# A graph layer's streamed table in six buffers of four blocks instead of three of five, with 12 instead of 16 buffers for gathered rows

## The chip, the cores and the metric

The kernel runs on one core of one Trainium2 chip. The metric is the device time of one execution in microseconds. Before the change, three runs gave 1752.2, 1746.14 and 1751.6 us, a median of 1751.6 us.

The engines are named as the profile names them: PE is TensorE (PEld its weight loads), DVE is VectorE, ACT is ScalarE, POOL is GpSimd, SP is SyncE, which here only issues DMAs.

## What is computed

There are 12,500 nodes with 128 features and 200,000 edges, sorted by destination; every edge has one of four types. The reference, cut to what matters:

```python
h = jnp.maximum(_layernorm(x, axis=-1), 0.0)
xs = h[src]
msgs = jnp.zeros((xs.shape[0], W.shape[2]), dtype=x.dtype)
for i in range(W.shape[0]):
    mask = (edge_type_4 == i)[:, None]
    msgs = msgs + jnp.where(mask, xs @ W[i] + b[i], 0.0)
out = x + jax.ops.segment_sum(msgs, dst, num_segments=N)
```

## The kernel before

**The table.** The first 110 us normalize x and write h into a table `htab` in DRAM, as three bf16 parts per value, so that a row has 384 bf16 (768 bytes). Partition p of a tile holds 98 consecutive rows (NW = 98), and "block j" is row j of all 128 partitions: 128 x 128 values in three parts, 98,304 bytes. The rows of x are loaded in 33 spans of up to three blocks by `load_span` (L472). Its tiles come from the pool `rows` (L234, 16 buffers of 1,536 bytes per partition). `load_span` is asked up to 13 spans ahead of the one that is normalized (L1240).

**Two kinds of edges.** The edges are cut into 1,563 chunks of 128. The first 512 chunks go to the few destinations with many edges and are treated as dense work. The other 1,051 go through gathers.

- *Gathered chunks.* For each chunk POOL issues one indirect DMA that fetches 128 rows of `htab` (L544). Two chunks share a tile `hm` of the same pool `rows` (HG = 2). Chunks are worked in groups of 16: `gather` (L538) asks for the rows of the next group while `sum_up` (L569) multiplies those of the present one (L578, three matmuls per chunk), sums by weights (L605), and DVE adds the result into a ring in SBUF (L666). The first 48 chunks take another path (rows of x itself, L528), so 1,003 gathers go through `rows`.
- *Dense work.* Destinations are handled in 18 batches: the first of 17 triples of nodes, then 17 of 27 triples. `count` (L940) counts, for a batch, how often each row of the table is a source: DVE makes one-hots (L959, L967), PE multiplies them (L985), ACT copies the finished count of each triple out of PSUM (L991). `multiply` (L1024) then multiplies the counts of the batch with the whole table: 98 blocks of three matmuls (L1040).

**The stream.** `multiply` reads the table from DRAM once per batch, HB blocks to a DMA on SP (L1032), into the pool `hsp` of STREAM buffers (L1290). With HB = 5 that is 20 DMAs per batch, 19 of 480 KB and one of 288 KB, 360 in all. Besides waiting for its buffer, each DMA is made to wait for a copy of `count`: the first ACT copy that PE's order puts behind the last matmul on that buffer.

```python
for j0 in range(0, NW, HB):
    j1 = min(j0 + HB, NW)
    hs = hsp.tile([P, HB, D3], BF16, name="hs")
    one = nc.sync.dma_start(hs[:, : j1 - j0, :], htab.rearrange("(p j) f -> p j f", j=NW)[:, j0:j1, :])
    free = [by for n, by in left_at if n > by_blocks[0] - STREAM]
    if free and by_blocks[0] >= STREAM:
        held_by(one, free[0], "the buffer of the stream is free")
```

`by_blocks` counts the buffers that PE is through with, and `left_at` holds each copy with the value of `by_blocks` at which it was emitted.

**The order.** From group 3 on, the order on PE, DVE and ACT is written out by hand (L1311 to L1400). Between two pairs of gathered chunks, `pace` (L1088) hands out steps of the dense work so that all groups have about the same number of matmul columns. `dense_work` (L1103) runs the count of a batch beside the multiplication of the batch before; multiplication is kept 15% behind (BEHIND, L1122), so at the end of a batch the last blocks run without a count beside them, and a new batch begins with 15% of its count before its first block of the other is multiplied:

```python
done = {st: 0.0 for st in steps}
while done:
    st = min(done, key=lambda st: done[st] + led.get(st, 0.0))
    part = next(st, None)
```

`multiply` yields after every block whatever HB is. POOL and SP each work through their own queue in order.

Of the kernel before, what the change touches and what calls it, by code (L numbers as in the profile page):

```python
# [55 lines left out]
C0 = 512  # L56
UB = 27
MANY = 16
HB = 5
SLOTS = 4  # L60
SETS = 4
STREAM = 3
BEHIND = 0.15
RING = 2048
OT = 4
# [9 lines left out]
def kernel(  # L75
# [155 lines left out]
    flag = const.tile([P, 1], I32, name="flag")  # L231

    mid = ExitStack()
    hpool = mid.enter_context(tc.tile_pool(name="rows", bufs=16))  # L234
    opool = mid.enter_context(tc.tile_pool(name="onehots", bufs=2))
    spool = mid.enter_context(tc.tile_pool(name="typed", bufs=2))
    x_ps = mid.enter_context(tc.tile_pool(name="x_ps", bufs=4, space=PSUM))
# [279 lines left out]
    def held_by(one, by, reason):  # L517
        tc.add_manual_dep(
            one.ins,
            by.name,  # L520
            mybir.DependencyInfo(mybir.DependencyClass.Sync, mybir.DependencyReason.DATA),
            reason=reason,
        )
# [14 lines left out]
    def gather(t0, g):  # L538
        got = []
        for h0 in range(0, g, HG):  # L540
            hm = hpool.tile([P, HG * D3], BF16, name="hm")
            for i in range(h0, min(h0 + HG, g)):
                at = (t0 + i) % (TURN * P)
                one = nc.gpsimd.indirect_dma_start(  # L544
                    out=hm[:, (i - h0) * D3 : (i - h0 + 1) * D3],
                    out_offset=None,
                    in_=htab,
                    in_offset=bass.IndirectOffsetOnAxis(ap=srcf[:, at : at + 1], axis=0),
                )
                if i == h0 and gates and t0 + i >= SOON:  # L550
                    held_by(one, gates.pop(0), "the first rows come while the slots are made, not ahead of them")
            got.append(hm)
        return lambda i, c: got[i // HG][:, (i % HG * 3 + c) * D : (i % HG * 3 + c + 1) * D]
# [470 lines left out]
    def multiply(vs, counts):  # L1024
# [3 lines left out]
        pa = a_ps.tile([P, 512], F32, name="pa")  # L1028
# [7 lines that stand above are left out]
# [253 lines left out]
    nc.vector.memset(o2s[:, :, :, NB:], 1.0)  # L1289
    hsp = counting.enter_context(tc.tile_pool(name="hsp", bufs=STREAM))  # L1290
    raw_sums = outp.tile([P, OT, D], F32, name="xo").rearrange("p j d -> p (j d)")[:, : RAW * G * win_raw]
# [14 lines left out]
    rows = gather(RAW * G, G)  # L1306
# [6 lines left out]
    for gi, (t0, g) in list(enumerate(zip(starts, sizes)))[RAW:]:  # L1313
# [11 lines left out]
        if gi < final:  # L1325
            rows = gather(starts[gi + 1], sizes[gi + 1])
# [203 lines left out]
```

## Time and profile before

The profiled execution took 1744.29 us; its span from the first to the last instruction is 1742.5 us. Its mean granted TensorE clock is 0.926.

| part of the span, us | what runs |
|---|---|
| 0 to 112 | x is normalized, the table is written, slots for the dense work are made |
| 112 to 190 | the first 48 chunks, the first count |
| 190 to 1690 | gathered groups, with count and multiplication between them |
| 1690 to 1742 | last groups, results leave |

| engine | busy us (share) | instructions |
|---|---|---|
| PE | 1435.4 (82%) | 10984 |
| DVE | 1015.9 (58%) | 5305 |
| ACT | 450.0 (26%) | 1095 |
| POOL | 1031.1 (59%) | 1078 |

The view of the costliest groups of instructions gives a line, engine and operation, its number, the busy time and mean duration of one, then the idle time of the engine just before them and what ended it. The view of waits gives, for each pair "who <- whom", the idle time in total, how many times, and the longest. "issue" there is idle time for whose end the profile shows no event. The chain that ended last follows the work back from the last instruction; "SPq" is SP issuing a DMA.

### The profile page before, as it was taken

Reading aid. Unit: us, or ns where it says so; the run is one execution under the profiler, and the core shown is the slowest. Engines: PE = TensorE matmul, PEld = TensorE weight load, DVE = VectorE, ACT = ScalarE, POOL = GpSimd, SP = SyncE. Lnnn points to the kernel's source line nnn. Section 1 sums busy time; section 2 is a strip of 40 time slices with the busy share of each in tenths; the row PEclk is TensorE's granted clock in tenths of the full one; section 3 lists DMA queues with packets and bytes.
Section 4 is the critical chain, followed back from the end, with each engine's and each line's share of the span. In section 5 each row is a group of like instructions: output and inputs, shape, how many; then the busy total and the mean of one; then the engine's idle time right before and its main releaser. Section 6 shows DMA issues by size and latency. Waiting matters only on the chain.

```text
span 1742.5 us, 32539 instructions
## 1 busy us (share of the span) xinstructions
PE 1435.4 (82%) x10984; PEld 938.3 (54%) x10984; DVE 1015.9 (58%) x5305; ACT 450.0 (26%) x1095; POOL 1031.1 (59%) x1078
## 2 busy tenths in 40 slices
PE   3876779787979787888888889888888989889875
PEld 1345565554656455555555555555555556555554
DVE  6972867565565556574647555756564556555334
ACT  5783322121212121212121222222222222122011
POOL 6536656565656565656665656666656566656561
PEclk8976799998999899999999999999999899999997
DMA  6542466565646465666555555655555655556652
GB/s 204 179 146 81 144 196 188 173 208 169 196 158 206 158 197 169 206 187 193 175 188 189 175 183 174 200 181 187 178 190 169 197 173 189 173 179 188 196 185 67
DMA packets 144538, 308.92 MB, mean 177 GB/s; under 512 B 26762, under 2 KB 77372, under 8 KB 144365
## 3 DMA queue, kind: packets, MB, share of 16 engines
q1 hardware_dynamic: 94685, 204.98, 35.9%
q0 software_dynamic: 49680, 101.81, 19.9%
q8 instruction: 86, 1.41, 0.3%
q14 instruction: 87, 0.71, 0.1%
HBM read 290.65 MB, written 16.04 MB: 176 GB/s over the span
## 4 chain that ended last, share of the span: by engine, by line
PE 52%; issue 19%; DMA 14%; DVE 5%; another core or an unknown queue 4%; ACT 4%; SPq 2%; DVEq 0%; ACTq 0%
PE pa L1040 27%; DMA hs<-htab 14%; PE pt L985 8%; PE py L605 5%; PE ps L578 4%; ACT counts L991 2%; PE pt L1056 2%; SPq L1032 1%; PE ps L635 1%; DVE oh L561 1%; PE py L596 1%; PE pt L691 1%; DVE o L967 1%; ACT sb L581 1%
## 5 line engine op out<-in xcount | busy, mean ns | idle before, releaser
L544 POOL DMA_INDIRECT hm<-htab,srcT x1003 | 974.6, 972 | 642.5 <-issue 227.1
L1040 PE MATMUL pa<-counts,hs 128*128 128x324 fp8e4 (+1 forms) x5292 | 970.4, 309 | 195.1 <-DMA hs<-htab 150.7
L1040 PEld LDWEIGHTS <-hs 128*128 128x128 bf16 x5292 | 490.9, 98 | 478.1 <-DMA hs<-htab 187.3
L959 DVE TENSOR_SCALAR o<-iota_n,hkT 128x392 bf16<-128x392 f16 x1167 | 381.3, 327 | 97.7 <-PE pt L985 44.1
L985 PE MATMUL pt<-o,o 128*128 128x396 bf16 x1167 | 374.9, 345 | 23.2 <-issue 10.4
L991 ACT CAST counts<-pt 128x396 int32<-128x396 f32 x476 | 230.0, 493 | 555.8 <-PE pt L985 306.3
L561 DVE TENSOR_SCALAR oh<-iota_b,keyT 128x56 bf16<-128x56 bf16 (+8 forms) x1003 | 171.5, 258 | 328.9 <-PE py L596 89.8
L581 ACT COPY sb<-ps 128x224 f32<-128x224 f32 (+8 forms) x251 | 99.7, 397 | 529.4 <-PE ps L578 237.5
L666 DVE TENSOR_TENSOR ring<-ring,py 128x14 f32 (+7 forms) x976 | 171.2, 175 | 82.5 <-PE py L605 20.8
L578 PEld LDWEIGHTS <-hm 128*128 128x128 bf16 x3009 | 166.1, 100 | 75.3 <-issue 30.1
L578 PE MATMUL ps<-oh,hm 128*128 128x56 bf16 (+8 forms) x3009 | 189.3, 199 | 18.0 <-issue 13.9
L967 DVE TENSOR_SCALAR o<-iota,loT 128x128 bf16<-128x128 bf16 x644 | 175.2, 272 | 0.0
L985 PEld LDWEIGHTS <-o 128*128 128x128 bf16 x1167 | 114.0, 99 | 77.3 <-issue 23.9
L967 DVE TENSOR_SCALAR o<-iota,loT,byT 128x128 bf16<-128x128 bf16 x417 | 139.6, 335 | 0.0
L605 PE MATMUL py<-sb,wsb 128*128 128x224 f32 (+7 forms) x488 | 130.3, 410 | 0.4 <-issue 0.3
L605 PEld LDWEIGHTS py<-sb,wsb 128*128 128x128 f32 x488 | 89.9, 197 | 24.6 <-issue 2.2
L528 POOL DMA_INDIRECT hx<-in_x_dram,srcT x48 | 50.9, 1060 | 34.1 <-issue 12.1
L1000 DVE COPY bi<-counts 128x27 int32<-128x27 int32 (+1 forms) x18 | 4.2, 232 | 106.0 <-issue 62.0
L600 ACT CAST cnt<-py 128x224 bf16<-128x224 f32 (+7 forms) x61 | 24.1, 395 | 112.4 <-PE py L596 35.2
L461 ACT ACTIVATE h<-hm,nmrt,rstdt 128x128 f32<-128x128 f32 x98 | 42.7, 492 | 2.2 <-DVE vart L446 1.9
L1056 PEld LDWEIGHTS pt<-sd,wsb 128*128 128x128 f32 x144 | 31.3, 304 | 6.9 <-ACT sd L1052 4.8
L1056 PE MATMUL pt<-sd,wsb 128*128 128x81 f32 (+1 forms) x144 | 31.0, 379 | 4.7 <-ACT sd L1052 4.7
(234 smaller groups left out, 639.6 us busy)
## 6 DMA issues: line engine op xcount, KB each, us to landing
hs<-htab SPq DMA_DIRECT2D x342, 480.0 KB
hm<-htab,srcT POOLq DMA_INDIRECT x1003
htab<-h SPq DMA_DIRECT2D x32, 288.0 KB
xo<-in_x_dram SPq DMA_DIRECT2D x23, 256.0 KB
out_dram<-xo SPq DMA_DIRECT2D x23, 256.0 KB
hs<-htab SPq DMA_DIRECT2D x18, 288.0 KB
hm<-in_x_dram SPq DMA_DIRECT2D x18, 192.0 KB
hm<-in_x_dram SPq DMA_DIRECT2D x14, 168.0 KB
```

What stands on the lines that cost most here:

```text
L544: one = nc.gpsimd.indirect_dma_start(out=hm[:, (i - h0) * D3 : (i - h0 + 1) * D3], out_offset=None, in_=htab, in_offset=bass.IndirectOffse ...
L561: nc.vector.tensor_scalar(oh[:, i, :], iota_b[:, :K], keyf[:, at : at + 1], None, ALU.is_equal)
L578: nc.tensor.matmul(ps[:, i - i0, :], rows(i, c), oh[:, i, :], start=(c == 0), stop=(c == 2))
L581: nc.scalar.copy(sb[:, i0:i1].rearrange("p g t n -> p g (t n)"), ps[:, : i1 - i0, :])
L605: nc.tensor.matmul(py[:, :g, :], wsb[:, t, :], sb[:, :g, t, :], start=False, stop=(t == NT - 1))
L666: nc.vector.tensor_tensor(to, to, of(i), ALU.add)
L959: one = nc.vector.tensor_scalar(o2[:, k, :NB], iota_n, hkT[:, s : s + 1], None, ALU.is_equal)
L967: one = nc.vector.tensor_scalar(o1[:, k], iota_1, loT[:, s : s + 1], by, ALU.is_equal, ALU.mult)
L985: one = nc.tensor.matmul(pb, o1, o2, start=first, stop=last)
L991: one = nc.scalar.copy(counts[:, :, i * NT : (i + 1) * NT], pb.rearrange("p (b t) -> p b t", t=NT))
L1040: nc.tensor.matmul(pa[:, : 3 * nu * NT].rearrange("p (m v) -> p m v", m=3), hs[:, j - j0, c * D : (c + 1) * D], of, start=(j == 0 and c == 0),
L1056: nc.tensor.matmul(py[:, : 3 * nu], wsb[:, t, :], sd[:, : 3 * nu * NT].rearrange("p (v t) -> p v t", t=NT)[:, :, t], start=(t == 0), stop= ...
```

## The change

The stream's DMAs carry four blocks instead of five, and there are six buffers for them instead of three: 25 DMAs per batch (24 of 384 KB, one of 192 KB), 450 in all. The room in SBUF per partition goes from 3 x 3,840 = 11,520 to 6 x 3,072 = 18,432 bytes. The pool `rows` has 12 buffers instead of 16, 18,432 bytes instead of 24,576: it holds 24 gathered chunks, or 12 spans of x, where it held 32 chunks or 16 spans. `STREAM` also enters the choice of the copy that a DMA waits for.

```diff
-HB = 5
+HB = 4
 SLOTS = 4
 SETS = 4
-STREAM = 3
+STREAM = 6
...
     mid = ExitStack()
-    hpool = mid.enter_context(tc.tile_pool(name="rows", bufs=16))
+    hpool = mid.enter_context(tc.tile_pool(name="rows", bufs=12))
```

## The prediction

> **What bounds the kernel now.** I read the stretch from 190 to 1690 us first, in the view of busy time by stretch (sum, then PE, PEld, DVE, ACT and POOL, granted clock, DMA share, GB/s):
>
> ```profile
> 190.00:1690.00 1500.00, 1278.01 (x10221) 845.74 (x10220) 869.01 (x4610) 330.51 (x786) 913.85 (x941) 0.95 0.58 185
> ```
>
> PE is busy for 1278 of 1500 us, DVE for 58%, POOL for 61%, the DMA engines for 58%. PE is near its bound, with 222 us idle. The waits of PE in that stretch say what for (total, times, longest):
>
> ```profile
> PE pa L1040 <- DMA hs<-htab: 150.7, 88, 8.1
> PE pa L1040 <- issue: 40.3, 46, 4.6
> PE ps L578 <- issue: 11.1, 23, 1.0
> PE pt L985 <- DVE o L967: 7.6, 3, 4.1
> ```
>
> In the trace, 180.1 us of the idle time lie directly before the first matmul on a stream buffer: the first row and most of the second. The other 42 us lie elsewhere. So the stream makes PE wait, and SP's own waits say why its DMAs come late:
>
> ```profile
> SPq L1032 <- ACT counts L991: 633.3, 146, 12.1
> ```
>
> The DMA waits for the copy that it is tied to. The chain shows it at the start of a batch (start us, duration, what):
>
> ```profile
> 665.47 1.51 PE pt L985 x9
> ...
> 668.70 0.39 ACT counts L991
> 669.09 0.02 issue
> 669.11 3.54 DMA hs<-htab
> ```
>
> The last matmul of the old batch is done at 665.47; the DMA of the next block is issued only after the new batch's first copy, at 669.11, and lands at 672.65, when PE has long run out of counting.
>
> Over all full buffers after the first 20 the trace gives these means: last matmul on a buffer to issue of the DMA that refills it 3.98 us, issue to first packet 1.36 (0.95 with nothing ahead), packets 2.24, then about 0.4 to the matmul. That is 8.0 us. With three buffers a refill has the time of two others, 2 x 1500/360 = 8.3 us. There is nothing to spare, so each late copy stalls PE.
>
> **The clock.** Of these 1500 us, 139.9 are granted at half rate, in 28 stretches. Their lengths are multiples of 3.4 us, and in the 3.4 us before each PE was idle for half of the time or more. PE worked 112 us in them, which at full rate is 56 us less; 48 us of this belongs to the 25 stretches where the idle time was a wait for the stream.
>
> The Trainium skill (TensorE: Matmul & The Clock Gate, section "HAM oscillation — how this bites in real kernels") says that gaps of over about 3.4 us are to be avoided; by it only the 13 stream waits of over 3.4 us would cost clock, by my estimate one half-rate window each, 13 x 3.4 / 2 = 22 us, and the sum below would be 26 us higher. The trace differs: the half-rate stretch at 471.2 follows a wait of 2.8 us, so I take the rows.
>
> **The change, part by part.** It is summed against the profiled execution (span 1742.5, time 1744.3).
>
> *Six buffers of four.* A refill now has the time of five others. Without its waits and the slow clock the stretch takes about 1500 - 180 - 48 = 1272 us, 2.83 us per buffer, so 14.1 us. It needs 4.0 + 1.4 + 2.24 x 4/5 + 0.4 = 7.6 us. The 6.5 us left cover most late copies (nine in ten refills now begin within 6.8 us of the release). So -180 for the waits and -48 for the clock. PE's order is the same, as `multiply` yields per block.
>
> *Starts of batches.* Counting ends when multiplication is at 85%, 83 of 98 blocks, so 20 buffers are through at the last copies. A DMA of the next batch needs a copy with at least 20, 21, 22 ... for its first, second, third buffer. So the first is free early; the second to sixth wait for the new batch's first copy, as the first three do now. By the times above, the second would be issued at 669.1 and be there at 669.1 + 0.95 + 1.8 + 0.4 = 672.2, while PE starts the first buffer by 668.7 and takes some 3 us for it (5.7 for five blocks here, at a slow clock in part): about 0.5 us late, 17 times, +9. Bounds: 0, and the present waits of some 4.5 us (+75).
>
> *90 more DMAs on SP.* An issue takes 0.32 us at the median: 450 take 144 us of 1500. SP waits for most of the stretch; nothing is added. A run of packets begins while the one ahead ends, so the 0.95 us is paid only with an empty queue.
>
> *Gathers with 12 buffers.* POOL now stays 32 chunks ahead: a gather begins 44 to 54 us before its matmul, and is held only by its buffer:
>
> ```profile
> POOL hm L544 <- issue: 212.2, 687, 0.6
> POOL hm L544 <- PE ps L578: 190.2, 107, 6.8
> ```
>
> With 24 chunks at 1.33 us (1272 us for 955) it begins some 29 us ahead, after 2 to 4 us from release to gather. Stream DMAs land within 5 us of issue even with two ahead of them; gathered rows are a fifth as large. The lead is ample. What grows is POOL's load: a gather takes 1.25 us from start to start when nothing holds it (0.95 and 0.30 of issue; mean 1.27), so POOL's 979 gathers after its first 24 take 1241 us, from 150 us on to about 1391, while PE gets to the end of the batches at about 1470. POOL is over 90% occupied and not quite the bound: +5, bounds 0 and +75 (below).
>
> *The tail.* From 1689 on, PE uses chunks 1008 to 1050 in 40 us, faster than POOL makes them. The last gather now begins at 1709.7 and is used at 1729.1. With 24 chunks, the gathers from the 1010th's release (1697.4) on run without a break: 1699 + 17 x 1.25 = 1720, landed by 1725. It still fits; 0.
>
> *Loads of x with 12 buffers.* Span u + 13 now takes the buffer of span u + 1, which is not yet normalized when it is asked for; with 16 it was that of u - 3, done before. On SP the store of span u - 2 may stand behind that load. ACT takes the store's buffer back five spans later and spans follow each other every 2.2 to 4 us, DVE is busy for 48.5 of the 50 us from 50 to 100, and the loads end with span 32. So +2; bounds 0 and +15 (21 such loads by 0.7 us, the longer issue there).
>
> *DVE and ACT* keep their work in less time: DVE goes to 68%. PE waits 7.6 us for one-hots now; +5, bounds 0 and +40 (a fivefold).
>
> Sum: 1742.5 - 180 - 48 + 9 + 5 + 2 + 5 = 1535.5, and 1.8 around the span: 1537. The median of the runs is 1751.6 where the profiled execution took 1744.3, 0.4% more, so I forecast 1544 us. Own range: 1523 without any of the additions; about 1612 with one of the two bounds of +75 taken whole.
>
> **The rivals.**
>
> - *POOL becomes the bound* (1,633 us). If PE catches up with the gathers and each pair is handed over anew, a pair takes 2.5 us and the shortest hand-over seen, 0.41: 490 pairs, 1426 us, from 150 to 1576, then some 50 us of tail and the 0.4%. For it: the load of over 90%. Against it: all gathers are ahead by dozens of chunks. 10%.
> - *The copies hold the stream still* (1,641 us): it doesn't do what it says, since every DMA is still tied to a copy, and at a batch's start five of six wait for the same one. The present waits at starts, about 4.5 us x 17 = 76, and 30 us of clock would stay: 1544 - 9 + 106. Against it: the fourth to sixth are needed 6 us and more after the first copy. 7%.
> - *Transfers go one at a time* (1,662 us). 450 x (0.95 + 1.79 + 0.4) = 1413 us from 190, then 52, and the 0.4%. Against it: the packets of buffer 124 begin at 687.00 us, those of 123 end at 687.13, so they overlap. 4%. The Trainium skill (DMA: Bandwidth & Descriptors, section "Anatomy of one DMA") gives some 2.0 us for each DMA beside its bytes, for those issued from POOL, which speaks against smaller pieces; by it, as an estimate, 450 x 2.9 us = 1305 would give about 1554.
> - *The gathers slow down* (slower than before, some 1,890 us). If denser work on DVE and the DMA engines lengthens a gather, POOL sets the end: 979 times its cadence. From 1.58 us on ((1742.5 - 195) / 979) the kernel is slower than now; at the 1.72 us that a gather and its wait take together from 200 to 250 us (29 in 50 us) it would be 150 + 1684 + 50 = 1884 and the 0.4%. For it: a gather lasted 1.2 us and more here and there. Against it: the median is 1.25 us in every stretch, with the DMA share at 0.71 (200 to 250 us) as at 0.52. 3%.
> - The forecast: 76%.
>
> **The numbers.** The range goes from 1495, where a part of the 42 us of other idle time goes too, to 1640: it holds the forecast's own range and POOL as the bound, some 84%. About 0.5% is what a measurement of this kernel can tell from no change. Faster by over 0.5%: 0.96 (all but the last rival and a little); within: 0.01; slower: 0.03.
>
> **What would show it.** Right: PE's wait at L1040 for hs under 30 us in all, the clock at 0.97 or more from 190 us to the end of the batches, PE's work there near 1225 us, a gather still 25 to 35 us ahead, stores of the table finished by 115 us. Wrong: PE waiting at L578 for DMA hm (POOL is the bound); waits at the first buffers of each batch (the copies hold); PE waiting at L985 for DVE; or the table later by more than 10 us.

## The result, and the profile after

The kernel after took 1671.46 us (median of four runs, 1668.77 to 1675.38), the kernel before 1751.9 us beside it: ratio 0.9535, 95% interval 0.9482 to 0.9587. It is faster by 80 us, where 207 were forecast, and lies outside the range. The profiled execution took 1675.38 us, its span is 1673.5 us, and the granted clock rose from 0.926 to 0.949.

First the stretch of the batches, in the same view of busy time by stretch (us, then PE, PEld, DVE, ACT, POOL, clock, DMA share, GB/s):

```profile
190.00:1600.00 1410.00, 1249.12 (x10065) 817.88 (x10064) 857.63 (x4555) 325.19 (x777) 899.77 (x924) 0.98 0.62 194
```

The clock is what I forecast (0.98, where 0.97 or more was said), and yet PE is idle for 161 of 1410 us. The waits of PE in that stretch (190 to 1620 us; total, times, longest) say for what:

```profile
PE pa L1040 <- issue: 68.8, 125, 5.5
PE ps L578 <- issue: 35.9, 61, 1.2
PE pt L985 <- issue: 17.9, 34, 1.2
PE pt L985 <- DVE o L967: 12.3, 9, 4.1
...
PE pa L1040 <- DMA hs<-htab: 4.3, 4, 2.3
```

The reader is to see two things. The wait for the stream, 150.7 us before, is 4.3: that step went as forecast. And the rows with "issue", waits for whose end the profile shows no event, are now the large ones: 68.8 us at L1040 and 35.9 at L578, against 40.3 and 11.1 before. In the chain that ended last the DMAs all but vanish (before: PE 52%, issue 19%, DMA 14%):

```profile
PE 77%; issue 11%; DVE 7%; ACT 2%; another core or an unknown queue 1%; DMA 1%; SPq 0%; DVEq 0%; ACTq 0%
```

For an account that adds up, I took from the trace the time from the first product (L1040) to the last, and split PE's idle time by what the matmul behind it waited for. "Pause" is idle time ahead of a matmul that waits for no semaphore.

| us | before | after | forecast change | change |
|---|---|---|---|---|
| first to last L1040 | 1498.7 | 1431.0 | -209 | -68 |
| waits for the stream | 182.0 | 20.1 | -171 | -162 |
| other waits, and pauses | 38.0 | 140.0 | +10 | +102 |
| of these, pauses | 26.7 | 95.1 (200 of them) | | +68 |
| PE busy | 1277.8 | 1269.6 | -48 | -8 |
| at half clock | 144.4 | 53.3 | | -91 |

So the stream's waits went, and two thirds of their time came back in other places.

PE's busy time has to be taken apart too, because a row of PE is longer than the time that its matmul adds. Rows of L1040 last 0.30 us, but at full clock and without a stop they start every 143 ns, before and after alike (medians; 32 ns at L578). So the row ahead of every stop counts some 160 ns in which PE may already stand. With each matmul put at the spacing that it has at full clock without a stop (means from e5 and e11), PE's work is the same in both kernels, and this is what its busy time holds beyond it:

| us | before | after | change |
|---|---|---|---|
| work at full clock | 1191.1 | 1191.1 | 0 |
| added by the half clock | 50.8 | 22.7 | -28 |
| rows ahead of stops | 31.4 (196 stops) | 50.2 (314 stops) | +19 |
| the rest | 4.4 | 5.6 | +1 |

The question for the chip was what the pauses are.

### The profile page after: what moved, and what is told of

The parts are those of the page before. It is cut to its first block, busy times and chain, and to the rows that moved or that the text cites. A ratio compares the mean times of both kernels' runs of the same rounds, so it can differ in the third digit from the quotient of the medians.

```text
span 1673.5 us, 32746 instructions
## 1 busy us (share of the span) xinstructions
PE 1428.9 (85%) x10984; PEld 925.3 (55%) x10984; DVE 1014.6 (61%) x5305; ACT 448.9 (27%) x1095; POOL 1031.2 (62%) x1078
## 4 chain that ended last, share of the span: by engine, by line
PE 77%; issue 11%; DVE 7%; ACT 2%; another core or an unknown queue 1%; DMA 1%; SPq 0%; DVEq 0%; ACTq 0%
PE pa L1040 44%; PE pt L985 11%; PE py L605 7%; PE ps L578 7%; DVE o L959 2%; DVE o L967 1%; PE pt L1056 1%; PE ps L635 1%; PE pt L691 1%; DVE oh L561 1%; PE py L596 1%; DVE ring L666 1%; PE ps L490 1%; DMA hs<-htab 1%
## 5 line engine op out<-in xcount | busy, mean ns | idle before, releaser
L1040 PE MATMUL pa<-counts,hs 128*128 128x324 fp8e4 (+1 forms) x5292 | 961.9, 305 | 77.1 <-issue 68.8
L1040 PEld LDWEIGHTS <-hs 128*128 128x128 bf16 x5292 | 492.5, 97 | 349.7 <-issue 123.2
L959 DVE TENSOR_SCALAR o<-iota_n,hkT 128x392 bf16<-128x392 f16 x1167 | 385.5, 330 | 79.3 <-PE pt L985 33.6
L985 PE MATMUL pt<-o,o 128*128 128x396 bf16 x1167 | 372.4, 342 | 36.8 <-issue 20.5
L991 ACT CAST counts<-pt 128x396 int32<-128x396 f32 x476 | 229.9, 495 | 470.6 <-PE pt L985 172.0
L578 PE MATMUL ps<-oh,hm 128*128 128x56 bf16 (+8 forms) x3009 | 193.1, 197 | 45.4 <-issue 38.9
L578 PEld LDWEIGHTS <-hm 128*128 128x128 bf16 x3009 | 165.1, 98 | 111.1 <-issue 66.4
L985 PEld LDWEIGHTS <-o 128*128 128x128 bf16 x1167 | 112.1, 98 | 96.9 <-issue 34.2
L490 PE MATMUL ps<-h,ident 128*128 128x384 f32 (+1 forms) x34 | 19.9, 676 | 16.0 <-issue 12.5
L1056 PE MATMUL pt<-sd,wsb 128*128 128x81 f32 (+1 forms) x144 | 25.1, 332 | 6.8 <-ACT sd L1052 5.4
```

Of the source, the lines that this page charges most:

```text
L578: nc.tensor.matmul(ps[:, i - i0, :], rows(i, c), oh[:, i, :], start=(c == 0), stop=(c == 2))
L959: one = nc.vector.tensor_scalar(o2[:, k, :NB], iota_n, hkT[:, s : s + 1], None, ALU.is_equal)
L985: one = nc.tensor.matmul(pb, o1, o2, start=first, stop=last)
L991: one = nc.scalar.copy(counts[:, :, i * NT : (i + 1) * NT], pb.rearrange("p (b t) -> p b t", t=NT))
L1040: nc.tensor.matmul(pa[:, : 3 * nu * NT].rearrange("p (m v) -> p m v", m=3), hs[:, j - j0, c * D : (c + 1) * D], of, start=(j == 0 and c == 0),
```

## Experiments

Eighteen kernels ran, on six chips that differ: the same kernel before took 1526 us on one and 1773 on another. Every ratio is to the kernel before on the same chip. A letter for a theory holds for its group of runs only (I of e1 to e3 is not I of e17).

### e1 to e4: the obvious suspects (chip with 1773 us for the kernel before)

In e1 the stream is not read again; in e2 a third of the products is split in two; in e3 a third of the gathered rows' matmuls is left out; e4 is the kernel before with 12 buffers for rows.

```diff
-            hs = hsp.tile([P, HB, D3], BF16, name="hs")
-            one = nc.sync.dma_start(hs[:, : j1 - j0, :], ...)
+            hs = hs_all[:, j0 // HB % STREAM * HB : (j0 // HB % STREAM + 1) * HB, :]
```

> The changed kernel, but the table is not streamed: 24 of its 98 blocks are loaded once and used over and over, so the multiplication with blocks 24 to 97 of the table is replaced by that with blocks 0 to 23. PE's instructions are the same. In the changed kernel PE is idle for 161 us between its first and last L1040: 20 before stream buffers, 45 at other instructions with a wait, 95 at instructions that wait for no semaphore. Theory I (PE is short of instructions: its sequencer can't keep the array fed once the stream waits no longer give it time to run ahead): only the 20 us and little else go, 1,640 to 1,665 us, idle without a wait still 80 us or more. Theory D (the denser stream of DMAs holds PE up, in its reads or its instruction fetch): idle without a wait falls under 35 us, as before the change, 1,570 to 1,600 us.

Measured: 1688.89 us, ratio 0.9524 (0.9473 to 0.9576), the same as the change itself, above the ranges of both theories. Pauses 124.9 us, half clock 50.1 us. The stream is off the path, and its transfers do not make the pauses.

```diff
+                    for m0, m1 in ((0, 2), (2, 3)) if c == 1 else ((0, 3),):
```

> The changed kernel with one in three of the L1040 matmuls (part c = 1) split into one of two thirds and one of a third of the columns: the same columns, 1,764 more pairs of weight load and matmul. Theory I: an instruction costs some 60 ns of PE's sequencer (842 of them in the densest 50 us), so 1,764 x 2 x 60 ns = 210 us more work for it, of which little is hidden: 1,780 to 1,880 us. If PE's array is the limit (theory D, or waits on DVE): 1,764 further pairs of up to 30 ns, 1,670 to 1,730 us.

Measured: 1709.39 us, ratio 0.9634 (0.9582 to 0.9687). By the two ratios the 1764 more matmuls cost some 17 us against the change itself, 10 ns each; as the kernel after did not run on this chip, that is uncertain by some 13 us. The time lies in the range of the other theory; theory I, which expected 1,780 us and more, is out: the supply of instructions is not what bounds PE.

```diff
-                for c in range(3):
+                for c in range(2):
```

> The changed kernel without the third part of the gathered rows (L578 does two matmuls per chunk instead of three): 1,003 pairs of short matmuls fewer. The array needs some 32 ns for one (the median from start to start). Theory I: 2,006 instructions of some 60 ns less, 1,003 x 120 ns = 120 us, at least half of it won: 1,550 to 1,610 us. Array as the limit: 32 us less, 1,630 to 1,650 us.

Measured: 1685.38 us, ratio 0.9498 (0.9446 to 0.9549); pauses 105.9 us, 129.7 us at half clock. In neither range: 1003 matmuls fewer gain about 6 us, which is within the intervals. Theory I is out. But the run does not show that PE's work costs nothing: in the account above, the matmuls left out are worth 30 us, near the 32 of the other theory, and the longer time at half clock adds 30 us more than in the kernel after (52.8 against 22.7).

```diff
-    hpool = mid.enter_context(tc.tile_pool(name="rows", bufs=16))
+    hpool = mid.enter_context(tc.tile_pool(name="rows", bufs=12))
```

> The kernel before with 12 row buffers instead of 16 and nothing else. By the prediction +2 us, 1,745 to 1,760 us, POOL 20 to 35 us ahead. Rival: the row buffers cost a part of the missing gain in the changed kernel, and so here too: 1,765 us or more, with PE waiting at L578.

Measured: 1766.23 us, ratio 0.9968 (0.9941 to 0.9995): the buffers taken from the rows cost nothing, as forecast.

### What the trace shows of PE's ends

In the timeline of the kernel after (start us, duration, what, and in brackets the engine's idle time before it), ACT's copy L991 waits for nothing but the last L985 of its count, which by its row ends at 736.13:

```profile
735.80 0.33 PE L985 MATMUL pt<-o,o 128*128 128x396 bf16 x1
...
738.26 0.45 PE L1040 MATMUL pa<-counts,hs 128*128 128x324 fp8e4 x2 [0.51 <-issue]
738.29 0.49 ACT L991 CAST counts<-pt 128x396 int32<-128x396 f32 x1 [3.45 <-PE ps L578]
739.69 0.30 PE L1040 MATMUL pa<-counts,hs 128*128 128x324 fp8e4 x1 [0.98 <-issue]
```

ACT has been idle for 3.45 us and starts at 738.29, and the record of PE's semaphore is at 738.27: 2.14 us after the modelled end. Over 250 to 1300 us, PE's semaphore comes 0.87 us after the end of the nearest matmul before it that signals (median; a tenth over 2.27 us). For ACT and DVE this delay is 9 and 11 ns. So PE's rows show when a matmul is taken up, and the signal that it is done comes up to microseconds later; PE runs on for a dozen matmuls and then stands, waiting for no semaphore. Whether the results themselves are late, or their signals alone, the trace doesn't show; "results held up" below stands for both. The Trainium skill (Perfetto Trace Analysis, section "Tensor Engine Instruction (MATMUL, LD_WEIGHTS)") says that the end of a matmul in a trace is estimated and not observed; the trace agrees, with these 0.87 us.

### e5 to e8: PE alone, no gathers, no one-hots, four buffers (chip with 1526 us for the kernel before)

```diff
+        for kinds in ["a"] * 1200 + ["s"] * 1536 + (["a"] * 3 + ["o"] + ["a"] * 4 + ["o"] + ["a"] * 4 + ["s"] * 6 + ["o"]) * 60:
+            pair(kinds)
```

> The kernel after, with three bursts of TensorE pairs put behind its end; they read constant tiles, wait for no semaphore, and write six banks of their own that nobody reads: 1200 pairs of the shape of the product's (324 columns), 1536 of the shape of the gathered rows' (40 columns), and 60 times the mix of a pair of chunks (11 of 324, 3 of 396, 6 of 40 columns). Theory A (the array's own cost: the 40-column pairs need more time than the 28 to 32 ns that lie between their records, a weight load each, and the pauses without a semaphore are the array catching up): the second burst takes 50 to 80 ns a pair, and the mix takes over 2.45 us each time, with pauses of 0.2 to 1 us in it. Theory H (the pauses are handed over by another engine, GpSimd's gathers before all): 143 ns, 28 to 32 ns, and 2.25 us (11 x 143 + 3 x 165 + 6 x 30) without a pause.

Measured (one execution): 144.3 ns, 27.7 ns and 2.227 us, without a pause in the mix. But the part ahead of the bursts, the kernel after itself, has no pauses either: first to last L1040 takes 1213.4 us, and its work ends at 1414 us. The kernel after has 5.6 us more of span behind its last work, and 1.8 around the span, so it would take some 1421 us here (an estimate): against 1526 a ratio of 0.93, of one execution. PE's semaphores come 13 ns after the modelled ends on this chip.

```diff
+            if len(kept) == 11:
+                took[0] += 1
+                got.append(kept[took[0] % 11])
+                continue
```

> The kernel after, without its gathers of table rows from the 23rd chunk on: TensorE reads the rows of the first 22 chunks again and again (what is left out: the gathering of all other rows). TensorE's and VectorE's instructions stay. Theory H (GpSimd's gathers cause the pauses, by their instruction, their packets or their hand-over of buffers): of the 95 us of pauses without a semaphore most go, TensorE's span falls by 70 to 100 us, ratio to before about 0.90 to 0.915. Theory A (the array's own cost): the pauses stay at 80 to 110 us, ratio 0.945 to 0.96. A third, V (VectorE's one-hots pace the loop): the same as A.

Measured: 1411.39 us, ratio 0.9249 (0.922 to 0.9278), no pauses. As the kernel after has none here, this tells nothing of the theories.

```diff
+                if at >= SETS:
+                    yield o1[:, k], o2[:, k], None
+                    continue
```

> The kernel after, with the one-hots of the slots made for the first four sets alone and read again for all others (what is left out: some 2500 VectorE instructions, 0.5 us for two, and the counts are not those of the edges). TensorE's instructions stay. Theory V (VectorE's one-hots pace the loop, behind the waits and the pauses alike): the 45 us of waits and most of the 95 us of pauses go, ratio 0.87 to 0.90. Theories A and H: only the waits of TensorE on VectorE go, some 20 to 40 us, and the pauses stay, ratio 0.93 to 0.945.

Measured: 1385.76 us, ratio 0.9075 (0.9046 to 0.9103). There are no pauses here either, so this tells nothing of them. PE is idle for 3.0 of 1193.7 us: this is the time of PE's work alone, and VectorE's part of the kernel after (1213.4 us) is under 20 us on this chip.

```diff
-STREAM = 6
+STREAM = 4
...
-    hpool = mid.enter_context(tc.tile_pool(name="rows", bufs=12))
+    hpool = mid.enter_context(tc.tile_pool(name="rows", bufs=16))
```

> Four buffers of four blocks for the stream (six in the kernel after), 16 buffers of gathered rows as before. If depth four is enough to hide the transfer, the waits for the stream stay under 40 us and the ratio is within 0.01 of that of the kernel after, 0.945 to 0.965; if six buffers are needed, the waits for the stream are 80 to 150 us and the ratio is 0.97 to 0.995.

Measured: 1486.93 us, ratio 0.9765 (0.9717 to 0.9813), with 54.2 us of waits for the stream and 44.4 us at half clock, against 2.0 and 10.2 in e5's part. The waits lie between the two forecasts. Four buffers of four are not enough; six are.

### e9 to e12: both kernels, no gathers and PE alone once more (chip with 1768 us for the kernel before)

e9 and e10 are the two kernels unchanged, e11 is e6 again, e12 is e5 again.

> The kernel before, unchanged, for its profile beside that of the kernel after on one chip. Theory C (the pauses without a semaphore come from the chip that runs the kernel: two chips so far gave 1752 and 1773 us for the kernel before and 95 to 137 us of pauses in the others, a third gave 1526 us and none): where the kernel before takes about 1526 us, its profile has under 5 us of pauses and 80 to 120 us of waits for the stream; where it takes over 1740 us, 20 to 40 us of pauses and 170 to 210 us of waits for the stream.

Measured: 1773.04 us, ratio 1.0018 (0.9985 to 1.0051); stream 195.0 us, pauses 24.2 us. As theory C has it.

> The kernel after, unchanged. Theory C: where the kernel before takes about 1526 us, this one takes 1405 to 1425 us (ratio 0.92 to 0.935), with under 5 us of pauses without a semaphore and under 10 us of waits for the stream; where it takes over 1740 us, the ratio is 0.945 to 0.96 again, with 80 to 125 us of pauses. Against theory C (the pauses come and go by the execution, on any chip): the profile has pauses of 20 us or more on a chip with a fast kernel before, or none on a slow one.

Measured: 1696.62 us, ratio 0.9582 (0.9531 to 0.9634); pauses 105.9 us. As theory C has it.

> The kernel after without its gathers of table rows from the 23rd chunk on, once more. On a chip with pauses it tells theory H (GpSimd's gathers bring the pauses out there: they go, ratio 0.90 or less) from the others (80 us of pauses or more stay, ratio 0.94 to 0.96). On a chip without pauses: the same as e6, ratio 0.92 to 0.93.

Measured: 1424.43 us, ratio 0.8042 (0.7987 to 0.8098), on the chip with pauses. Theory H holds. The batches with gathers (e10), by stretch:

```profile
183.60:1632.70 1449.10, 1274.51 (x10220) 833.34 (x10219) 865.78 (x4605) 326.68 (x784) 914.16 (x939) 0.98 0.61 190
```

and without (e11):

```profile
176.00:1382.00 1206.00, 1195.93 (x10217) 824.44 (x10216) 836.30 (x4603) 338.84 (x782) 0.00 (x0) 1.00 0.49 152
```

The same matmuls (the bracket behind PE's busy time counts them) take 243 us less. The idle time falls from 175 to 10 us, and the busy time by 79 us. By the account above, 24 of these are the half clock (60 to 5 us of it) and 51 the rows ahead of stops (335 stops against 16). The waits for the stream that were left fall too, from 25.6 to 1.4 us.

> The kernel after with the three bursts behind its end, once more. On a chip with pauses it tells whether TensorE pauses by itself (theory A there: pauses in the bursts, over 30 ns a pair in the second or over 2.4 us a time in the third) or only beside the other engines' work (theory H: 144 ns, 27.7 ns and 2.23 us, as on the chip without pauses).

Measured (one execution): 144.8 ns, 26.9 ns and 2.227 us with no pause in the mix, behind a kernel with 103.2 us of pauses. PE by itself does not pause on this chip.

### e13 to e16: what of a gather (chip with 1543 us for the kernel before)

The four replace the gather, or a part of it. This chip held nothing up: PE's semaphores came after 14 ns in all four, also in e14 and e15, which still gather by index. So they told nothing of the cause.

```diff
-                one = nc.gpsimd.indirect_dma_start(...)
+                one = nc.gpsimd.dma_start(hm[...], htab.rearrange("(p j) f -> p j f", j=NW)[:, (t0 + i) % NW, :])
```

> The kernel after, with each gather of 128 rows by index replaced by a plain DMA of 128 rows of the table, issued by GpSimd in the same place, with the same bytes, tiles and waits (left out: the choice of rows by index). Theory S (the gather's own path: descriptors that GpSimd writes, and its software queue, hold up TensorE's completions): on a chip with pauses they go, under 15 us, ratio 0.80 to 0.84. Theory D (the data that land in SBUF) and theory W (GpSimd's waits on TensorE's semaphore): they stay, 70 to 130 us, ratio 0.93 to 0.97.

Measured: 1414.17 us, ratio 0.9177 (0.9106 to 0.9248).

```diff
-            for i in range(h0, min(h0 + HG, g)):
+            for i in range(h0, h0 + 1):
```

> The kernel after with every second gather left out: TensorE reads the rows of the chunk before twice. Theories S and D, if the cost is per gather: half of it, TensorE's span from its first to its last product some 1330 us on a chip with pauses (1449 with all gathers, 1206 with none), ratio 0.87 to 0.89. Theory W: GpSimd waits as often for buffers and longer, so the pauses stay: 1400 us or more, ratio over 0.92.

Measured: 1415.23 us, ratio 0.9184 (0.911 to 0.9258).

```diff
-            got.append(hm)
+            got.append(kept[:, took[0] % 2])
```

> The kernel after with all its gathers, but into tiles that TensorE does not read, while it reads the rows of the first four chunks again and again (left out: the use of the gathered rows); GpSimd then never waits for TensorE. Theory W (GpSimd's waits on TensorE's semaphore bring the pauses): the pauses go, span 1206 to 1230 us, ratio 0.80 to 0.83. Theories S and D: the gathers run as long as there are any and hold TensorE up as before, pauses of 70 us or more, ratio 0.92 to 0.96.

Measured: 1420.17 us, ratio 0.9216 (0.9145 to 0.9287).

```diff
-                one = nc.gpsimd.indirect_dma_start(...)
+                for c in (0, 1):
+                    one = nc.gpsimd.memset(hm[...], 0.5 + c)
```

> The kernel after with each gather replaced by two GpSimd instructions that set the same part of the tile to a constant (left out: the gathered rows); GpSimd is busy, writes the tiles itself and waits for TensorE as before, and no DMA runs for it. Theory W, or one that lays the pauses on GpSimd's work as such: they stay, 70 to 130 us on a chip with pauses, ratio 0.92 to 0.97. Theories S and D: they go, under 15 us, ratio 0.80 to 0.84.

Measured: 1442.24 us, ratio 0.9359 (0.9284 to 0.9434); 20.5 us at half clock.

### e17 and e18: all ways in one kernel

```diff
+        way = "index" if n < 12 else "plain" if n < 22 else "sync" if n < 32 else "set" if n < 42 else "index" if n < 52 else "unread"
```

> The kernel after with ten buffers of gathered rows, and another way of filling them in each stretch of groups of 16 chunks: gathers by index (groups 1 to 12), the same bytes by plain DMAs of GpSimd on its software queue (13 to 22), by plain DMAs of SyncE on the queue of the stream (23 to 32), GpSimd sets them to a constant (33 to 42), gathers by index again (43 to 52), gathers by index into tiles that nobody reads (the rest; TensorE reads the first four chunks again). Left out: the rows themselves in all but the stretches by index. The measure is by how much TensorE's semaphore comes after the modelled end of its matmul, median in each stretch: 14 ns without a hold-up, 0.4 to 0.9 us with it so far. On a chip with pauses: theory S (GpSimd's software queue) expects over 0.3 us by index, plain on GpSimd and unread, under 0.05 us on SyncE and set; theory D (data that land in SBUF) over 0.3 us in all but the set one; theory W (GpSimd waits on TensorE's semaphore) over 0.3 us by index, plain and set, under 0.05 us on SyncE and unread; a fifth, I (the index alone: rows from scattered places of the table), over 0.3 us by index and unread alone. On a chip without pauses: 14 ns in all.

Measured (one execution, 1759.79 us for the kernel before): this chip pauses. Stretches by index, plain on GpSimd, plain on SyncE, set, index, unread, in the view by stretch (us; PE, PEld, DVE, ACT, POOL; clock, DMA share, GB/s):

```profile
250.00:400.00 150.00, 132.59 (x1104) 86.42 (x1103) 95.71 (x502) 35.11 (x90) 96.82 (x99) 1.00 0.64 197
450.00:600.00 150.00, 147.46 (x1265) 100.87 (x1263) 108.80 (x601) 40.21 (x98) 62.91 (x115) 0.99 0.72 222
620.00:780.00 160.00, 159.64 (x1372) 109.42 (x1368) 108.99 (x600) 47.04 (x111) 0.00 (x0) 1.00 0.76 229
860.00:1010.00 150.00, 148.34 (x1243) 101.21 (x1242) 121.45 (x580) 42.47 (x97) 101.69 (x232) 1.00 0.48 145
1060.00:1240.00 180.00, 163.03 (x1245) 105.57 (x1244) 98.23 (x522) 43.95 (x101) 115.46 (x120) 0.96 0.62 187
1320.00:1440.00 120.00, 30.73 (x115) 12.28 (x114) 10.74 (x54) 4.26 (x9) 87.17 (x92) 0.54 0.34 95
```

Read PE against the length of the stretch. PE's semaphores come after 0.99 us, 13 ns, 14 ns, 13 ns, 0.93 us and 2.7 us (medians; the last of ten records). Theory I holds, in one execution with a control at both ends: it is the gather by index, and neither its bytes nor its queue nor GpSimd's work or waits. More data per us move in the plain stretches (222 and 229 GB/s) than in those by index, and nothing is held up there. In the last stretch gathers run back to back, 1.25 us from start to start with one break of 5.3 us, and PE all but stops: 115 matmuls in 120 us. What follows shows the link best. In the next 20 us, with 16 gathers, PE gets 7 matmuls done. After the gather at 1460.2 us none begins until 1528.4; PE is back at its pace by some 1476, and does 165 matmuls in 20 us:

```profile
1440.00:1460.00 20.00, 2.02 (x7) 0.73 (x7) 0.00 (x0) 0.00 (x0) 15.14 (x16) 0.50 0.30 79
1480.00:1500.00 20.00, 20.00 (x165) 13.90 (x163) 13.85 (x74) 6.21 (x13) 0.00 (x0) 1.00 0.34 106
```

Theory W had it the wrong way round. In the kernel after, GpSimd pauses for over 0.4 us between gathers in 21% of the time (it waits for PE to release a tile), and 56% of PE's semaphores come in these pauses; on the chip of e5, where it hardly pauses, they are spread evenly.

```diff
+        way = "index" if n < 12 else "rows" if n < 22 else "half" if n < 32 else "two" if n < 42 else "index" if n < 52 else "set"
```

> The kernel after with another way of gathering in each stretch of groups of 16 chunks: by index as it is (groups 1 to 12), by index with 128 consecutive rows of the table as the index (13 to 22), by index for every second chunk alone, TensorE reading each of these twice (23 to 32), by index for the first 64 rows and by a plain DMA of GpSimd for the other 64 (33 to 42), by index as it is (43 to 52), set to a constant by GpSimd (the rest). Left out: the right rows in all but the stretches by index as it is. The measure is again the median time from the modelled end of TensorE's matmul to its semaphore. On a chip with pauses, by index as it is 0.6 to 1.2 us and set 14 ns. If the scattered addresses hold TensorE up: consecutive rows under 0.05 us. If the instruction by index does: consecutive rows 0.6 to 1.2 us as well. If it goes with the instructions: half of them 0.1 to 0.6 us, those of 64 rows 0.6 us or more; with the rows: both 0.1 to 0.6 us. If TensorE gets on only while GpSimd pauses (e17 had it almost stopped where GpSimd never waited): with half of the gathers, where GpSimd waits half of the time, under 0.05 us.

Measured (one execution): 1489.81 us on a chip with 1524.43 us for the kernel before, 14 ns in every stretch. It told nothing; whether the addresses or the instruction by index hold PE up, and by instruction or by row, stays open.

## Why the prediction was wrong

Its mechanism was right, and it is not the whole. By its steps:

- *Waits for the stream, -180 +9 at the starts of batches:* right. They went from 182.0 to 20.1 us, and e1 has nothing left to gain from the stream. At the starts 11.8 us lie ahead of the first two buffers of the batches, where 9 were forecast and some 76 would have stayed had the copies held the stream, so that rival fell. With so few waits, the rival of transfers one at a time fell too. e8 shows that the depth of six does it.
- *Clock, -48:* too large. The time at half clock fell from 144 to 53 us and the granted clock is 0.98, but the forecast left only 8 us of cost, and 22.7 stayed: the half clock gave 28 us instead of 48. PE's busy time fell by 8 us alone, since the 118 additional stops put 19 us of rows ahead of stops back into it. So this term was 40 us off, 20 by the clock and 20 by the step that follows.
- *"The other 42 us lie elsewhere", taken to stay:* **this is the step that failed.** They are 38 us by the account above, and became 140. They were not a fixed remainder but the visible part of a second limit: on this chip gathers by index hold PE's results up, as e11 and e17 show on two chips that behave like it. That much of it lay under the waits for the stream before the change is argued from this account, not shown: no run took the gathers out of the kernel before. 92 us of the miss are here (+102 where +10 were allowed for), and the 20 just named.
- *Gathers with 12 buffers, +5:* right, with e4 at 0.9968, and a gather still 28 to 41 us ahead of its matmul (29 forecast). POOL was not the bound in the sense of that rival: rows are never late. Its 1,633 us, and the 1,641 and 1,662 of the next two rivals, lie nearer to the result than the forecast by accident; the sign of this one, PE waiting at L578 for the rows, is absent.
- *Loads of x, +2:* the first product came 6.7 us earlier (190.24 to 183.55); the cause is open. *Tail, 0:* +5.3.
- *DVE and ACT, +5:* e7 gives under 20 us for all of VectorE's waits where nothing is held up; on this chip waits with a semaphore rose from 11.3 to 44.9 us, part of the 140.

The sum of the misses: 9 + 92 + 40 in the batches, and -3 outside, 138 us between the forecast span of 1535.5 and 1673.5.

None of the rivals was this one; "the gathers slow down" came near in its culprit, but it looked at the duration of a gather, 0.95 us then and now, and not at what a gather does to PE.

It could have been read before. In the view of the line L991 of the kernel before, its idle time (us, times) is put down to these:

```profile
  PE pt L985: 306.3, 169
  PE ps L578: 90.7, 47
  remote: 89.9, 36
```

The copy needs L985 alone. On the chip of e5, the kernel after has this instead:

```profile
  PE pt L985: 439.7, 397
  issue: 1.3, 1
  PE ps L578: 1.3, 1
```

A wait that ends long after its cause, so that the profile names a later matmul or "remote", is the sign that PE's results come late: 0.46 us in the median of the kernel before. The "late copies" that I took as the pattern of the work were in part that; in how large a part is not shown. How much of the 182 us of waits for the stream came from it was not measured; the kernel before costs 1526 us where nothing is held up, and the one after about 1421 by the estimate above. So there too the change gave about 105 us and not 207, and no trace of the kernel before on such a chip says how long its waits for the stream are.

No version here beats the kernel after without leaving work out.

## What to carry to other kernels

Removing the largest wait uncovers the next limit, so before counting on the whole of it, ask what the remaining idle time is and whether it lies under the wait. Take the end of a matmul from what its consumer does, not from its own row: idle time of a copy that is put down to the wrong matmul, and pauses of PE without a semaphore, belong together. When a theory on a pause cannot be told apart by removing work, put the candidates into one kernel, stretch by stretch, with a control at both ends.

## What was not expected of the hardware

- Gathers by index on GpSimd hold up TensorE's results on some chips. On the chips of the result, of e1 to e4, of e9 to e12 and of e17 the semaphore of TensorE comes 0.5 to 1.1 us late in the median while such gathers run; on those of e5 to e8, of e13 to e16 and of e18 13 to 14 ns. The kernel before takes 1752 to 1773 us on the former and 1524 to 1543 us on the latter.
- The price for the kernel after is 243 us of 1449 (e10 against e11; where nothing is held up, the gathers cost 9 us, 1213.4 against 1204.9 in e5's part and e6), and gathers back to back left PE 31 busy us of 120 (e17), with the clock at 0.54.
- Matmuls of 40 columns with a weight load each went at 27 ns a pair in a row of 1536 (e5, e12), and 1764 more matmuls cost some 17 us, give or take 13, while results were held up (e2).
